# A new order of the round and of the end in a layer-1 FFN laid out by hand over 32 images

## The chip, the cores and the metric

The kernel runs on one core of one Trainium2 chip. The metric is device microseconds (us) of one execution; lower is better. A core has TensorE (PE in the profile; its weight loads are PEld), VectorE (DVE), ScalarE (ACT), GpSimd (POOL) and SyncE (SP), each with its own instruction queue that runs strictly in order. Here SP only issues DMAs. An instruction that needs another engine's result waits on a semaphore, and everything behind it on its own queue waits too.

## The reference

A two-layer vision tower over 32 images of 256 tokens with 256 features. Everything ahead of the last stage (tokenizer, layer-0 attention and FFN, layer-1 attention) is the same in both kernels. The last stage, the layer-1 FFN, is what the change reorders. Cut to what matters, with B=32 images, 4 heads (NH) of width 64, and 4 experts (NE) per head:

```python
sx = einsum('bsh,ndh->bnsd', x, hl_w) + hl_b            # heads
q  = einsum('bnsd,neod->bneso', sx, wq)                 # four experts' queries per head
k, v = ...                                              # one key and value per head
att = softmax(q @ k.T * d**0.5 + causal)                # 16 attentions per image
out = att @ v
gs  = softmax(out . gate_w + gate_b)                    # gate over the four experts
mixed = sum over experts of out * gs
hn  = layernorm(mixed + resid)                          # first norm
hx  = relu(hn @ fc1_w.T + fc1_b) @ fc2_w.T + fc2_b      # first and second layer
hx  = layernorm(hx + hn)                                # second norm
fg  = softmax(hx . fgate_w)                             # gate over the four heads
h   = h + hx * fg
```

## The kernel before

All 32 images stay in on-chip memory from stage to stage. The layer-1 FFN takes one image at a time, but no engine finishes an image before it begins the next: the work of an image is cut into some 80 pieces (the tuple `PIECES`; pieces are named below by their function, in words), and `ROUND` lists all of them once, each with an offset. In round r the entry `(-k, p)` does piece p for image r + k. So entries with a large k belong to an image that has just come in, those with k = 1 to one about to leave. `order_e` walks the rounds in this order until piece 3 (`heads`) of image 31 has been done; from there on `END` lists every piece that is left, as `(images before the last, piece)`. Both lists are written out by hand or by a planner ahead of time; at run time nothing decides an order, and each engine runs the pieces that are its own in the order of the list.

The way of one image, with the engine of each step:

1. `features_in` (SP): DMA of the image's normed, turned features, tile exT. `heads` (PE), `heads_out` (ACT, tile sx, L1173), and two DMAs that swap its halves (sw, L1179).
2. `experts` 0 and 1, `head_values` (PE), evicted by ACT (tile g, L1206) and DVE (tile ev, L1221).
3. `scores` 0 to 4 (PE), each followed by `exponentials` of the same number (ACT, tile et, L1250, two instructions each).
4. `outputs` 0 to 3 (PE), evicted by `outputs_out` 0 to 7 (ACT, tile eo, L1285).
5. The gate over experts, `mixed`, `summed` (DVE, L1342 to L1394); `squares` 0 (ACT), `squares_sum` 0 (DVE, L1403), `root` 0 (ACT, a Ln and an Exp, L1410 and L1411), `scaled` (DVE, L1421).
6. The turn: `turn_e` transposes 32x32 blocks on DVE (tile eblk, L1428) and writes them to DRAM by DMA (er_turned, L1433); `moved_e` reads them back with two DMAs (fraw, L1440); `turned_e` scales them on ACT (fxT, L1449). Image 31 alone is turned on PE, without DRAM.
7. `first_layer` (PE, the turned rows' first product), `features_moved` (two DMAs fxT to both, L1461), `first_layer_out` (ACT, tile hx, L1487, then four DMAs hx to both, L1490), `second_layer` (PE), `second_layer_out` (DVE, tile ey, L1502).
8. `squares` 1, `squares_sum` 1, `root` 1; the head gate (`head_gate` 0 to 8, small DVE work with one ACT exponential); `last_norm` 0 to 2 (three full DVE passes, L1537 to L1541), 3 and 4 (four DVE instructions each, L1545), 5 (the DMA of the result, L1549). `heads_zero` and `features_zero` count zeros on DVE (L1184).

Eight PSUM banks are handed out in turn in the order of the list (`bank()`), so the ninth bank asked for is the first again, and the product that writes it waits until the engine that evicts the earlier content is done. One round asks for 29 banks. All DMAs of this stage go through SP's one queue in the order of the list; a DMA that has to wait holds back those behind it.

In the round before, `turn_e` of an image stands near the end of a round (entry `(-3, 66)`), `moved_e` opens the next (`(-2, 2)`), `turned_e` and `first_layer` follow in its first half (`(-2, 67)`, `(-2, 69)`) and `second_layer` closes it. `heads` stands just ahead of `second_layer`.

Of the kernel before, what the change touches and what calls it, by code (L numbers as in the profile page):

```python
# [80 lines left out]
def vit_tower(tc, a, out):  # L81
# [1032 lines left out]
    with (  # L1114
# [419 lines left out]
        def last_norm(b, im, i):  # L1534
# [38 lines left out]
            (features_moved,), (count_bad, 0), (count_bad, 1), (count_bad, 2), (count_bad, 3),  # L1573
        )
        ROUND = (
            (-2, 2), (-3, 54), (-1, 72), (-3, 56), (-4, 42), (-6, 4), (-1, 73), (-4, 33), (-1, 74), (-4, 34),
            (-4, 44), (-3, 57), (-4, 45), (-1, 75), (-3, 58), (-3, 59), (-6, 1), (-6, 5), (-4, 43), (-1, 76),
            (-4, 46), (-6, 6), (-5, 16), (-5, 12), (-5, 22), (-1, 77), (-6, 30), (-5, 18), (-2, 67), (-6, 9),
            (-1, 87), (-5, 13), (-4, 47), (-5, 14), (-2, 92), (-2, 69), (-6, 10), (-1, 78), (-5, 19),
            (-6, 11), (-1, 79), (-3, 60), (-4, 48), (-5, 20), (-3, 61), (-6, 7), (-5, 15), (-2, 68),  # L1580
            (-1, 80), (-2, 70), (-1, 89), (-3, 62), (-1, 81), (-4, 49), (-1, 82), (-6, 8), (-1, 88),
            (-3, 63), (-3, 64), (-1, 83), (-5, 31), (-1, 84), (-4, 50), (-5, 32), (-1, 85), (-1, 86),
            (-7, 3), (-8, 0), (-1, 90), (-3, 65), (-5, 21), (-4, 51), (-1, 91), (-5, 41), (-3, 66), (-5, 40),
            (-5, 39), (-4, 52), (-4, 53), (-4, 55), (-2, 71), (-1, 93), (-1, 94), (-1, 95), (-1, 96),
        )
        END = (
            (0, 2), (3, 51), (4, 65), (2, 40), (3, 52), (2, 39), (2, 42), (2, 41), (2, 21), (0, 1), (3, 53),
            (4, 66), (3, 54), (3, 55), (5, 71), (3, 56), (6, 90), (3, 57), (5, 72), (4, 2), (2, 33), (2, 34),
            (0, 4), (5, 73), (5, 74), (3, 58), (2, 43), (5, 75), (2, 44), (3, 59), (1, 15), (5, 76), (2, 46),
            (2, 45), (5, 77), (2, 47), (5, 78), (6, 91), (2, 48), (0, 7), (1, 21), (4, 67), (3, 60), (0, 9),  # L1590
            (2, 49), (3, 61), (4, 92), (2, 50), (5, 79), (4, 69), (0, 10), (0, 5), (0, 8), (2, 51), (3, 62),
            (2, 52), (5, 80), (0, 11), (5, 87), (2, 53), (3, 63), (1, 13), (4, 70), (3, 64), (2, 54),
            (5, 81), (2, 55), (4, 68), (1, 14), (5, 82), (2, 56), (3, 65), (0, 6), (5, 89), (3, 66), (2, 57),
            (1, 19), (1, 16), (1, 12), (1, 20), (0, 12), (5, 83), (5, 88), (4, 71), (1, 18), (1, 22),
            (2, 58), (0, 18), (4, 72), (3, 2), (4, 73), (2, 59), (4, 74), (4, 75), (1, 31), (1, 32), (1, 33),
            (1, 41), (1, 34), (1, 42), (1, 39), (1, 40), (4, 76), (3, 67), (2, 60), (5, 84), (0, 30),
            (5, 85), (3, 69), (2, 61), (5, 86), (5, 90), (1, 44), (3, 68), (0, 13), (1, 43), (2, 62),
            (1, 45), (2, 63), (3, 92), (1, 46), (5, 91), (3, 70), (0, 14), (1, 47), (4, 77), (0, 16),
            (2, 64), (1, 48), (4, 78), (1, 49), (4, 79), (1, 50), (4, 80), (1, 51), (2, 65), (1, 52),
            (1, 53), (4, 81), (2, 66), (0, 22), (0, 15), (4, 82), (0, 19), (1, 55), (1, 54), (0, 20),  # L1600
            (4, 87), (3, 71), (4, 83), (1, 56), (0, 31), (4, 89), (1, 57), (4, 84), (3, 72), (0, 21),
            (1, 58), (0, 32), (0, 40), (3, 73), (4, 85), (1, 59), (4, 88), (1, 60), (0, 41), (0, 42),
            (3, 74), (2, 2), (3, 75), (0, 39), (2, 67), (1, 61), (0, 33), (0, 43), (4, 86), (4, 90), (0, 34),
            (0, 44), (3, 76), (3, 77), (1, 62), (1, 63), (2, 69), (2, 92), (3, 78), (4, 91), (2, 68),
            (2, 70), (1, 64), (1, 65), (3, 79), (0, 46), (0, 45), (0, 47), (3, 80), (1, 66), (0, 48),
            (3, 81), (0, 49), (3, 87), (3, 82), (1, 2), (2, 71), (0, 50), (3, 83), (0, 51), (3, 89), (0, 52),
            (3, 84), (3, 88), (0, 53), (3, 85), (0, 55), (0, 54), (2, 72), (2, 73), (0, 56), (2, 74),
            (3, 86), (0, 57), (2, 75), (3, 90), (2, 76), (0, 58), (3, 91), (1, 67), (2, 77), (0, 59),
            (2, 78), (0, 60), (2, 87), (2, 79), (1, 92), (0, 61), (2, 80), (2, 89), (1, 69), (2, 81),
            (1, 70), (0, 62), (1, 68), (2, 82), (1, 71), (2, 83), (0, 63), (0, 64), (2, 84), (2, 88),  # L1610
            (2, 85), (0, 65), (0, 66), (2, 90), (1, 73), (0, 67), (1, 72), (2, 86), (0, 69), (0, 92),
            (1, 74), (1, 75), (2, 91), (0, 70), (0, 68), (0, 71), (0, 93), (0, 72), (0, 73), (0, 74),
            (0, 94), (1, 76), (0, 75), (1, 77), (0, 76), (0, 95), (1, 78), (0, 77), (0, 87), (0, 78),
            (1, 79), (1, 87), (1, 80), (0, 79), (0, 96), (1, 81), (0, 80), (1, 82), (1, 89), (1, 83),
            (0, 81), (0, 89), (0, 82), (0, 83), (1, 84), (1, 88), (0, 84), (1, 85), (0, 88), (0, 85),
            (1, 86), (1, 90), (1, 91), (0, 90), (0, 86), (0, 91),
        )
        LAST = PIECES.index((heads,))

# [407 lines left out]
```

## Time and profile before

| | us |
|---|---|
| median of 3 runs (1803.8 to 1807.66) | 1806.92 |
| the profiled execution, its own time | 1813.98 |
| its span, first to last instruction | 1812.2 |
| first product of `heads`, image 0 | at 1241.0 |
| the same, image 5 | at 1303.16 |
| the same, image 31, where `END` begins | at 1733.6 |
| last DVE instruction | ends at 1807.6 |

Busy shares of the whole span are PE 97%, DVE 72%, ACT 43%, POOL 25%. The layer-1 FFN is the last 571 us of the span, and the shares there differ from these, so it has to be read by its own stretches: the filling of the pipeline (1241 to 1303), 26 full rounds (to 1733.6) and the end. A matmul's end is modelled, so PE counts as busy while it waits a little; its pace is read from the starts of the products instead.

### The profile page before, as it was taken

To read this page: it belongs to the slowest core of one execution; us is meant where nothing else is said; L and a number is where in the kernel's file an instruction comes from. 1 tells how busy PE (TensorE), PEld (TensorE's weight loads), DVE (VectorE), ACT (ScalarE), POOL (GpSimd) and SP (SyncE) were. 2 spreads that over 40 slices of the span, in tenths; PEclk is the share of its full clock that TensorE was granted. 3 is DMA by queue.
4 is the path that set the end of the run, shared out by engine and by line. 5 is a ranking of instruction groups with operands and counts; after the bars stand their busy time and mean duration, and the time that the engine had idled before them with its cause. 6 is when DMAs were issued, how large, how long until landed. Compare 5 with 4: busy or idle time off the path is not lost.

```text
span 1812.2 us, 43832 instructions
## 1 busy us (share of the span) xinstructions
PE 1763.8 (97%) x18072; PEld 1267.4 (70%) x18072; DVE 1309.8 (72%) x3580; ACT 776.5 (43%) x1607; POOL 445.5 (25%) x506
## 2 busy tenths in 40 slices
PE   9999999999999999999999999999999999999993
PEld 7888566667576676767654555557888888888882
DVE  2335367787878665444458877875699999999998
ACT  0000322222222212121244554555888888888883
POOL 1223234343434335333344433341000000000000
PEclk9999999999999999999999999999999999999995
DMA  8552112121211115233312222112244444444432
GB/s 274 180 154 65 35 30 67 51 72 38 59 47 49 57 50 182 91 119 99 112 57 82 75 88 78 74 71 83 68 114 112 115 111 120 109 118 114 122 99 69
DMA packets 197999, 167.93 MB, mean 93 GB/s; under 512 B 71713, under 2 KB 174881, under 8 KB 197409
## 3 DMA queue, kind: packets, MB, share of 16 engines
q1 hardware_dynamic: 191072, 147.49, 28.4%
q0 software_dynamic: 6144, 16.79, 3.1%
q8 instruction: 144, 2.36, 0.6%
q10 hardware_dynamic: 576, 0.79, 0.2%
q14 instruction: 63, 0.51, 0.1%
HBM read 82.95 MB, written 57.41 MB: 77 GB/s over the span
## 4 chain that ended last, share of the span: by engine, by line
PE 85%; DVE 6%; DMA 4%; ACT 4%; issue 1%; SPq 0%; ACTq 0%; DVEq 0%
PE bank L118 85%; DMA er_turned<-eblk 1%; ACT et L1250 1%; DMA fraw<-er_turned 1%; DMA both<-hx 1%; DVE fout L1545 1%; ACT fxT L1449 0%; DMA patch<-in_patches_dram 0%; PE bank L518 0%; DVE eo L1380 0%; ACT g L1206 0%; DVE eblk L1428 0%; DVE ranges L1403 0%; DVE six L126 0%; ACT eo L1285 0%
## 5 line engine op out<-in xcount | busy, mean ns | idle before, releaser
L118 PE MATMUL bank<-ev,et 64*64 64x72 f32 (+3 forms) x6144 | 186.8, 226 | 0.2
L118 PEld LDWEIGHTS bank<-ev,et 64*64 64x64 f32 (+1 forms) x6144 | 171.6, 135 | 10.9 <-ACT hx L1487 1.2
L118 PE MATMUL bank<-tokW,patch 128*128 128x256 f32 x768 | 170.1, 385 | 2.9 <-DMA patch<-in_patches_dram 2.9
L118 PE MATMUL bank<-g,sw 64*64 64x128 f32 (+2 forms) x1280 | 168.0, 377 | 0.0
L1250 ACT ACTIVATE et<-bank 128x512 f32<-128x512 f32 x320 | 167.4, 624 | 1.2 <-PE bank L118 1.2
L118 PE MATMUL bank<-g,sx 64*64 64x128 f32 (+2 forms) x1280 | 167.6, 377 | 0.0
L118 PEld LDWEIGHTS bank<-tokW,patch 128*128 128x128 f32 x768 | 148.5, 194 | 24.9 <-issue 3.8
L118 PE MATMUL bank<-bxT,w_wuv 128*128 128x512 f32 x300 | 131.4, 592 | 0.0
L869 ACT ACTIVATE hT<-bank,cols 128x512 f32<-128x512 f32 x64 | 43.7, 687 | 187.2 <-PE bank L118 122.3
L118 PE MATMUL bank<-wvo,dm 128*128 128x512 f32 x256 | 114.3, 599 | 0.0
L118 PE MATMUL bank<-w_wo,gT 128*128 128x256 f32 x512 | 113.2, 379 | 0.0
L118 PE MATMUL bank<-attn,bv 128*128 128x256 f32 x512 | 113.1, 379 | 0.0
L118 PE MATMUL bank<-w_w,hT 128*128 128x256 f32 x512 | 112.3, 379 | 0.0
L118 PE MATMUL bank<-xsel,w_w 128*128 128x512 f32 x256 | 111.4, 592 | 0.0
L118 PEld LDWEIGHTS bank<-attn,bv 128*128 128x128 f32 x512 | 97.2, 190 | 19.6 <-issue 7.2
L126 DVE BATCH_NORM_STATS2 six<-h 128x6 f32<-128x256 f32 x256 | 105.7, 413 | 4.4
L118 PEld LDWEIGHTS bank<-w_w,hT 128*128 128x128 f32 x512 | 97.0, 190 | 15.6 <-issue 2.9
L118 PEld LDWEIGHTS bank<-w_wo,gT 128*128 128x128 f32 x512 | 97.2, 190 | 13.4 <-DVE gT L491 0.2
L118 PE MATMUL bank<-w_wuv,bxT 128*128 128x512 f32 x240 | 105.4, 592 | 0.0
L1285 ACT COPY eo<-bank 128x280 f32<-128x280 f32 x256 | 89.3, 396 | 36.4 <-PE bank L118 36.4
L118 PEld LDWEIGHTS bank<-bxT,w_wuv 128*128 128x128 f32 x300 | 57.0, 190 | 64.9 <-issue 64.1
L118 PEld LDWEIGHTS bank<-g,sx 64*64 64x64 f32 x1280 | 92.6, 133 | 10.1
(288 smaller groups left out, 3572.3 us busy)
## 6 DMA issues: line engine op xcount, KB each, us to landing
patch<-in_patches_dram SPq DMA_DIRECT2D x31, 768.0 KB
exT<-normed SPq DMA_DIRECT2D x32, 256.0 KB
sw<-sx SPq DMA_DIRECT2D x64, 128.0 KB
er_turned<-eblk SPq DMA_DIRECT2D x31, 256.0 KB
fraw<-er_turned SPq DMA_DIRECT2D x62, 128.0 KB
both<-fxT SPq DMA_DIRECT2D x62, 128.0 KB
both<-hx SPq DMA_DIRECT2D x124, 64.0 KB
out_dram<-fout SPq DMA_DIRECT2D x31, 256.0 KB
```

Of the source, the lines that this page charges most:

```text
L118: nc.tensor.matmul(o, lhsT, rhs, start=first, stop=last)
L126: nc.vector.bn_stats(six, x)
L869: nc.scalar.activation(s.hT[:, m, :], p, AF.Gelu_apprx_tanh, bias=col("b1", m))
L1250: nc.scalar.activation(t2[:, r, :], p, AF.Exp)
L1285: nc.scalar.copy(im.o[:, g * OC : (g + 1) * OC], p[:, 0:OC])
L1545: nc.vector.scalar_tensor_tensor(f[:, g, :], f[:, g, :], im.gate[:, i - 3, n : n + 1], H[b][:, i - 3, d], ALU.mult, ALU.add)
```

## The change

`ROUND` and `END` are replaced; no piece and no instruction is added, removed or changed in shape. Offsets now reach from -10 to -1 where they reached from -8 to -1: `features_in` is three rounds and more ahead, and the last part of an image (from the gate over heads on) ends one round later. The start of the list is another point of the same cycle; as a cycle, PE's pieces keep their order but for `heads`, which now stands ahead of `scores` 3 and `outputs` 0 and 1 instead of behind them. `turn_e` stands in the middle of a round (`(-4, 66)`), `moved_e` later in it (`(-4, 2)`), and `turned_e` and `first_layer` in the first quarter of the next (`(-3, 67)`, `(-3, 69)`).

```diff
         ROUND = (
-            (-2, 2), (-3, 54), (-1, 72), (-3, 56), (-4, 42), (-6, 4), (-1, 73), (-4, 33), (-1, 74), (-4, 34),
-            (-4, 44), (-3, 57), (-4, 45), (-1, 75), (-3, 58), (-3, 59), (-6, 1), (-6, 5), (-4, 43), (-1, 76),
-            (-4, 46), (-6, 6), (-5, 16), (-5, 12), (-5, 22), (-1, 77), (-6, 30), (-5, 18), (-2, 67), (-6, 9),
-            (-1, 87), (-5, 13), (-4, 47), (-5, 14), (-2, 92), (-2, 69), (-6, 10), (-1, 78), (-5, 19),
-            (-6, 11), (-1, 79), (-3, 60), (-4, 48), (-5, 20), (-3, 61), (-6, 7), (-5, 15), (-2, 68),
-            (-1, 80), (-2, 70), (-1, 89), (-3, 62), (-1, 81), (-4, 49), (-1, 82), (-6, 8), (-1, 88),
-            (-3, 63), (-3, 64), (-1, 83), (-5, 31), (-1, 84), (-4, 50), (-5, 32), (-1, 85), (-1, 86),
-            (-7, 3), (-8, 0), (-1, 90), (-3, 65), (-5, 21), (-4, 51), (-1, 91), (-5, 41), (-3, 66), (-5, 40),
-            (-5, 39), (-4, 52), (-4, 53), (-4, 55), (-2, 71), (-1, 93), (-1, 94), (-1, 95), (-1, 96),
+            (-1, 84), (-6, 22), (-4, 59), (-5, 47), (-3, 67), (-2, 75), (-4, 60), (-7, 9), (-5, 48),
+            (-6, 13), (-4, 61), (-3, 92), (-6, 18), (-7, 10), (-6, 14), (-5, 49), (-7, 11), (-3, 69),
+            (-4, 62), (-5, 50), (-5, 51), (-6, 19), (-1, 87), (-4, 63), (-7, 7), (-5, 52), (-8, 3), (-1, 85),
+            (-1, 89), (-3, 70), (-4, 64), (-5, 53), (-2, 76), (-1, 88), (-4, 65), (-4, 66), (-5, 54),
+            (-6, 20), (-7, 8), (-6, 15), (-1, 90), (-2, 77), (-1, 86), (-7, 30), (-5, 55), (-5, 56),
+            (-1, 91), (-6, 21), (-6, 31), (-8, 4), (-4, 2), (-2, 78), (-5, 57), (-6, 32), (-3, 71), (-6, 41),
+            (-6, 39), (-2, 79), (-2, 80), (-6, 33), (-3, 72), (-2, 81), (-3, 73), (-6, 40), (-10, 0),
+            (-6, 42), (-2, 82), (-3, 68), (-5, 58), (-6, 34), (-6, 43), (-6, 44), (-8, 1), (-8, 5), (-7, 16),
+            (-3, 74), (-6, 45), (-2, 83), (-7, 12), (-6, 46), (-8, 6), (-1, 93), (-1, 94), (-1, 95),
+            (-1, 96),
         )
         END = (
-            (0, 2), (3, 51), (4, 65), (2, 40), (3, 52), (2, 39), (2, 42), (2, 41), (2, 21), (0, 1), (3, 53),
...
-            (1, 86), (1, 90), (1, 91), (0, 90), (0, 86), (0, 91),
+            (0, 1), (7, 85), (7, 89), (1, 30), (5, 70), (4, 64), (3, 53), (2, 20), (7, 88), (4, 65), (1, 8),
+            (2, 15), (2, 31), (3, 55), (3, 54), (4, 66), (3, 56), (7, 86), (2, 32), (3, 57), (7, 90), (0, 4),
...
+            (1, 88), (1, 85), (0, 88), (0, 84), (1, 90), (0, 85), (1, 86), (0, 90), (1, 91), (0, 86),
+            (0, 91),
         )
```

`END` has 305 entries before and 332 after. The pieces that `END` holds more of than before are, on DVE: one `heads_zero`, one `features_zero`, one `last_norm` 0, two of `last_norm` 1, two of `last_norm` 2, one of `last_norm` 3, two of `last_norm` 4 and one set of the small head-gate steps; on PE: `scores` 3, `outputs` 0 and `outputs` 1 of one image.

The numbers of the pieces named most: 2 `moved_e`, 3 `heads`, 4 `heads_out`, 15 `scores` 3, 20 `exponentials` 2, 31 to 34 `outputs` 0 to 3, 64 and 76 `root` 0 and 1, 66 `turn_e`, 67 `turned_e`, 69 `first_layer`, 70 `first_layer_out`, 71 `second_layer`, 86 to 91 `last_norm`, 92 `features_moved`.

## The prediction

> **What bounds the kernel now.** I read the stretches of the last stage first, because shares of the whole span say nothing of it. Columns: stretch, length, busy us of PE, PEld, DVE, ACT, POOL with counts, granted clock, DMA share, GB/s.
>
> ```profile
> core 0: us, PE busy (x) PEld busy (x) DVE busy (x) ACT busy (x) POOL busy (x), PEclk, DMA share, GB/s
> 1241.00:1303.16 62.16, 60.97 (x1521) 53.47 (x1519) 34.91 (x96) 49.26 (x113) 2.40 (x4) 1.00 0.27 73
> 1303.16:1733.62 430.46, 426.14 (x10820) 363.58 (x10817) 409.36 (x1224) 361.73 (x911) 0.00 (x0) 1.00 0.44 114
> 1733.62:1812.20 78.58, 46.33 (x1016) 36.33 (x1012) 71.31 (x233) 40.83 (x106) 0.00 (x0) 0.75 0.31 84
> ```
>
> Two regimes. In the 26 full rounds PE sets the pace and DVE is close behind (409 of 430). In the end PE has 46 of 79 to do and DVE 71, and DVE's last instruction ends at 1807.6, 74 after the start: there DVE is the bound, with next to no idle time. So a microsecond of DVE work moved from the rounds into the end costs a microsecond.
>
> Next, how even the rounds are. The starts of `heads` lie 16.26 or 16.27 apart in the quiet rounds (1536.44, 1552.70), but 17.7 in others (1418.80 to 1436.49). 26 quiet rounds would take 422.9; they took 430.46: **7.6 us are stalls**. The chain of waits through one of the long rounds shows which:
>
> ```profile
> 1420.12 0.65 DVE eblk L1428
> ...
> 1420.79 5.02 DMA er_turned<-eblk
> ...
> 1425.83 0.62 SPq L1440
> ...
> 1426.50 3.62 DMA fraw<-er_turned
> ...
> 1430.22 0.82 ACT fxT L1449
> ...
> 1431.09 2.64 PE bank L118 x44
> ```
>
> From the end of the turn (1420.77) to fxT on ACT 9.45 pass, through two DMAs. ACT stood 1.32 at fxT and PE 1.02 behind it. In quiet rounds fxT starts at its place in ACT's queue with the data already there. ACT's queue allots 8.0 us from the end of the turn to fxT (1404.51 to 1412.48, 1337.66 to 1345.63); the slow cases take 8.5 to 9.5. SP's queue of this round shows why the first DMA was slow: two others of 256 KB stand just ahead of it.
>
> ```profile
> 1419.01 0.58 SPq L1144 DMA_DIRECT2D exT<-normed  x1
> 1419.69 0.48 SPq L1549 DMA_DIRECT2D out_dram<-fout  x1
> 1420.79 0.36 SPq L1433 DMA_DIRECT2D er_turned<-eblk  x1
> 1425.83 1.29 SPq L1440 DMA_DIRECT2D fraw<-er_turned  x2
> ```
>
> Last, ACT's queue in a quiet round, because the new order has to be laid against it. 1542.20 is where `outputs` 3 ends on PE.
>
> ```profile
> 1542.20 0.69 ACT L1285 COPY eo<-bank 128x280 f32<-128x280 f32 x2 [0.46 <-PE bank L118]
> ...
> 1543.51 1.07 ACT L1206 COPY g<-bank 128x512 f32<-128x512 f32 x2
> 1544.46 2.08 ACT L1250 ACTIVATE et<-bank 128x512 f32<-128x512 f32 x4
> 1546.38 0.86 ACT L1449 ACTIVATE fxT<-fraw,cols 128x512 f32<-128x512 f32 x1
> 1547.09 2.11 ACT L1250 ACTIVATE et<-bank 128x512 f32<-128x512 f32 x4
> 1549.00 0.93 ACT L1487 ACTIVATE hx<-bank,cols 128x256 f32<-128x256 f32 x2
> ```
>
> ACT runs without a break from 1542.2 to the end of hx at 1549.93, and `outputs` 0 (begun 1549.75) stops for 0.14 in its fourth product, whose bank that hx frees. So even the quiet round is held by this ACT chain through a bank, by a hair.
>
> **The change, part by part.** No instruction is added. What moves:
>
> 1. *The turn.* PE's work between `turn_e` and `first_layer` of an image grows by `scores` 3 and `outputs` 0 and 1: 0.97 and 2.95 by the starts (1548.78, 1549.75, 1552.70), 3.9 us. Measured from the end of `outputs` 3: DVE should finish the turn near 9.0, and fxT's place in ACT's new queue is 2.9 into the next round, at about 19.1, so 10.1 are allotted against the 9.5 of the slowest seen. On SP, exT and the 256 KB of the result now stand behind er_turned, not ahead; ahead of it stand the four hx DMAs (64 KB each, issued in 2.1 to 2.4), ahead of fraw the result and the two sw DMAs, all with work behind them that is not due for 5 us or more. `moved_e` waiting on SP holds back only `features_in`, due more than a round later. The four hx DMAs themselves gain: from hx to `second_layer` 5.1 are left where 4.7 were. I take all 7.6 of stall as gone in the profiled execution.
>
> [...]
>
> 2. *The round itself.* I lay ACT's new queue from the end of `outputs` 3, with starts back to back as in the rows above (et 0.478, g 0.477, hx 0.357, fxT 0.71, the square 0.52, Ln 0.35 and Exp 0.115): `outputs_out` 6 and 7, then `experts_out` 0 once PE is through at 1.0; 1.97 `exponentials` 4; 2.93 fxT; 3.63 `exponentials` 0; 4.59 the square; 5.11 `exponentials` 1; 6.07 the gate's Exp, 0.14; 6.20 hx; 6.92 `root` 0 and 1; 7.9 `exponentials` 2, whose first instruction ends at 8.55. PE is ready for `scores` 3 at 0.91 + 1.90 + 0.57 + 1.88 + 0.43 + 0.86 + 1.92 = 8.47 and needs the bank that this instruction frees. So the wait moves from `outputs` 0 to `scores` 3 and is about 0.1 again. From there PE needs 0.97 + 2.8 + 1.10 + 2.75 = 7.6 to the end of the next `outputs` 3: a round of 16.2, against 16.265. Bounds: PE alone, 16.1, and, should DVE hold up a `root` or the square, 16.5. I take 16.2: 26 x 0.065 = 1.7 us gained, between -4 and +6. DVE has 15.5 to do a round (409.36 over 26.5), and gets to what ACT waits for some 0.6 us ahead.
>
> 3. *The end.* At `heads` of image 31 PE has 3.75 less behind it than before (`scores` 3, `outputs` 0 and 1, pieces of 0.95 + 1.4 + 1.4), so `END` begins 3.75 earlier. But DVE has more in front of it: two zero counts (1.21), one `last_norm` 0 (0.60), two of 1 (1.20), two of 2 (1.29), three of 3 and 4 (12 x 0.196 = 2.35), head gate less one softmax step (0.65): **7.3 us**, all in the stretch that DVE bounds. The pace of the last kind, eight in 1.57 from start to start, is in the rows of the end:
>
> ```profile
> 1804.36 1.64 DVE L1545 SCALAR_TENSOR_TENSOR fout<-fout,fgate,h 128x64 f32<-128x64 f32 x8
> 1805.93 1.64 DVE L1545 SCALAR_TENSOR_TENSOR eblk<-eblk,fgate,h 128x64 f32<-128x64 f32 x8
> ```
>
> Nothing hides this: the work went out of the filling, where DVE is idle 44% of the time (34.9 busy of 62.2) and nobody gains by its having less. Net +3.5. On top come new waits of DVE: the one tile fout is free again only when the result of the image before has left; in the old end 3.1 us of DVE work lie between at the least, in the new one 2.6 and 2.9; and fxT of images 29 and 30 follow their turns by 8 to 9 us in ACT's queue with a square and a `root` behind them that DVE needs at once. I take 1.2, from 0 to 3.
>
> [...]
>
> 4. *The filling.* The same products in the same order: 0, give or take 1.
>
> **The sum** for the profiled execution: -7.6 - 1.7 - 3.75 + 7.3 + 1.2 = -4.6: its span 1812.2 becomes 1807.6, its own time 1809.4. It stands 7.1 above the median of 1806.92, about as much as its stalls, so the timed runs may hold fewer of them; nothing shows how many. I take 5.5 of 7.6, which makes -2.5: **1804.4 us**, a gain of 0.14%. A measurement of this kernel can tell about 0.2% (3.6 us) from no change, so the likeliest result lies just inside that band, which ends at 1803.3 and 1810.5.
>
> **The rivals.**
>
> *More is gained.* The bank wait falls away and PE's own 16.1 sets the round (-4.3 instead of -1.7), and the timed runs hold all the stalls: -3.75 - 7.6 - 4.3 + 8.5 = -7.2, 1799.8. For it: the stalls are seen in one round of three. Against: ACT's chain fits with nothing to spare.
>
> *The stalls belong to the profiled execution.* Timed runs hold 2: -2 - 1.7 + 3.5 + 1.2 = +1.0, 1808. For it: the 7.1. Against: the timed runs differ among themselves by 3.9 us, which something that varies must cause.
>
> *Slower: ACT's chain is late at `scores` 3.* `root` 0 and 1 now stand between hx and `exponentials` 2, each a Ln that its Exp must wait for, and `root` 0 needs a DVE sum that needs an ACT square. If DVE, at 95% busy, gets there 0.4 late, every round pays it. At a round of 16.56 it is +7.7 instead of -1.7: 1814. The sum without the round's gain is -0.8, so it decides (slower by over 3.6) from a round of 16.43 on, 26 x 0.17 = 4.4. Against: the 0.6 of lead.
>
> *It doesn't do what it says.* The wait at fxT stays, because SP issues er_turned late behind hx. Half of the stalls stay: 1807.
>
> **How the numbers follow.** The likeliest case 0.50 (own range 1801 to 1807.5, four tenths of it below 1803.3); more is gained 0.16; stalls of the profile alone 0.08; late at `scores` 3 0.19; the wait stays 0.07. Faster: 0.20 + 0.16 = 0.36. Slower: 0.19 and a little of the two small ones, 0.22. Same: 0.42. The range, from the gain's side to half of the slow case: 1799 to 1812.
>
> **What would show it.** fxT waiting for fraw gone from the waits of the rounds; rounds of `heads` even at 16.2; `scores` 3, not `outputs` 0, waiting for ACT et; 26 rounds in 421; `END` some 82 us from `heads` of image 31 to the last DVE instruction. It is wrong if rounds are above 16.4, or if the end takes under 78 or over 85.

## The result, and the profile after

The changed kernel takes 1802.12 us (median of 9 runs, 1800.96 to 1804.33), the kernel before on the same chip 1806.66 (9 runs, 1803.8 to 1809.64): a ratio of 0.9974, with a 95% interval of 0.9966 to 0.9982. That is 0.26% faster, inside the range given, 2.3 us below the predicted time, and just past the 0.2% line on the far side of which the likeliest case had been laid.

The last stage by stretches, as it was shown of before (stretch, length, busy us of PE, PEld, DVE, ACT, POOL with counts, granted clock, DMA share, GB/s), from `heads` of image 0, of image 5 and of image 31:

```profile
1237.40:1296.61 59.21, 58.02 (x1408) 48.91 (x1406) 32.91 (x91) 45.62 (x106) 2.40 (x4) 1.00 0.30 78
1296.61:1715.12 418.51, 418.40 (x10819) 352.53 (x10817) 400.94 (x1199) 358.30 (x909) 0.00 (x0) 1.00 0.45 116
1715.12:1799.70 84.58, 48.89 (x1128) 38.36 (x1126) 78.03 (x262) 44.72 (x117) 0.00 (x0) 0.79 0.31 84
```

The filling is 2.9 shorter, the 26 rounds are 11.9 shorter, and the end is 5.7 longer by its last DVE instruction (1794.79, which is 79.67 after the start of `END`; before 73.95). PE now fills the rounds to 418.40 of 418.51. Twenty-five rounds are 16.08 long and one is 16.51. The whole stage is 9.2 shorter up to its last DVE instruction. What is left behind that, the DMA of the last result, takes 4.9 where it took 4.6 (4.3 to 6.3 over all traces, in no relation to the change). Another 3.6 by which the profiled executions differ had gone before `heads` of image 0, in stages that the change doesn't touch.

The waits of the 26 rounds (engine and line, what it waited for, us in total, times, longest), first two of the kernel before:

```profile
ACT eo L1285 <- PE bank L118: 28.7, 52, 0.7
...
ACT fxT L1449 <- DMA fraw<-er_turned: 4.6, 6, 1.3
```

and then the changed kernel:

```profile
ACT eo L1285 <- PE bank L118: 45.5, 52, 1.6
...
PEld bank L118 <- ACT gate L1367: 10.0, 26, 0.4
...
PEld bank L118 <- ACT et L1250: 8.6, 26, 0.3
```

The row of fxT waiting for fraw is gone. ACT now waits 45.5 for `outputs` where it waited 28.7: it has become the engine that waits for PE. The third row looks like the wait that was forecast at `scores` 3. It will turn out to be none.

SP's queue in a quiet round, in which the turn ends at 1604.94:

```profile
1602.70 2.86 SPq L1490 DMA_DIRECT2D both<-hx  x4
1605.66 0.53 SPq L1433 DMA_DIRECT2D er_turned<-eblk  x1
1606.67 0.38 SPq L1549 DMA_DIRECT2D out_dram<-fout  x1
1607.58 1.11 SPq L1179 DMA_DIRECT2D sw<-sx  x2
1608.77 2.39 SPq L1440 DMA_DIRECT2D fraw<-er_turned  x2
1611.22 0.60 SPq L1144 DMA_DIRECT2D exT<-normed  x1
```

The order is as it was laid: er_turned is held back 0.7 by the four issues of hx, and the two DMAs of 256 KB now stand behind it. But fraw is not issued sooner: the result and the two sw DMAs, which wait for ACT's sx, stand ahead of it, and from the end of a turn to the issue of fraw 4.0 us pass in the middle case, where it was 3.1 in the kernel before. What keeps fxT from waiting here is the distance: from the end of a turn to fxT on ACT 10.06 pass in nearly every round, 2.1 more than before, without a gap on ACT.

In the end, two waits of those that had been expected (the first was 2.0 before, the second did not appear):

```profile
ACT fxT L1449 <- DMA fraw<-er_turned: 3.8, 1, 3.8
...
DVE fout L1537 <- DMA out_dram<-fout: 1.0, 1, 1.0
```

### The profile page after: what moved, and what is told of

The parts are those of the page before. It is cut to its first block, busy times and chain, and to the rows that moved or that the text cites. A ratio compares the mean times of both kernels' runs of the same rounds, so it can differ in the third digit from the quotient of the medians.

```text
span 1799.7 us, 43777 instructions
## 1 busy us (share of the span) xinstructions
PE 1753.4 (97%) x18072; PEld 1252.0 (70%) x18072; DVE 1300.9 (72%) x3580; ACT 773.5 (43%) x1607; POOL 444.4 (25%) x506
## 3 DMA queue, kind: packets, MB, share of 16 engines
q1 hardware_dynamic: 191072, 147.49, 28.7%
## 4 chain that ended last, share of the span: by engine, by line
PE 91%; DVE 6%; ACT 1%; DMA 1%; issue 0%; SPq 0%; DVEq 0%; ACTq 0%
PE bank L118 91%; DVE fout L1545 1%; DVE eo L1380 1%; DMA patch<-in_patches_dram 0%; DVE dx L842 0%; PE bank L518 0%; DVE six L126 0%; DVE ranges L1403 0%; ACT dex L950 0%; DVE dxB L199 0%; DVE two L1388 0%; DVE junk L1184 0%; DMA fraw<-er_turned 0%; DVE fout L1537 0%; DVE dz L996 0%
## 5 line engine op out<-in xcount | busy, mean ns | idle before, releaser
L118 PE MATMUL bank<-ev,et 64*64 64x72 f32 (+3 forms) x6144 | 181.5, 226 | 0.7 <-ACT et L1250 0.3
L1250 ACT ACTIVATE et<-bank 128x512 f32<-128x512 f32 x320 | 172.2, 600 | 4.3 <-PE bank L118 4.2
L1285 ACT COPY eo<-bank 128x280 f32<-128x280 f32 x256 | 84.8, 404 | 49.9 <-PE bank L118 49.9
L118 PEld LDWEIGHTS bank<-g,sw 64*64 64x64 f32 x1280 | 86.3, 133 | 15.2 <-ACT et L1250 9.0
```

The source lines that it names most:

```text
L118: nc.tensor.matmul(o, lhsT, rhs, start=first, stop=last)
L1250: nc.scalar.activation(t2[:, r, :], p, AF.Exp)
L1285: nc.scalar.copy(im.o[:, g * OC : (g + 1) * OC], p[:, 0:OC])
```

## The experiments

Each is compared with the kernel before on its own chip. "Trace" gives filling, 26 rounds and end (to the last DVE instruction) of one execution.

**How many stalls does an execution of before usually hold?** The kernel before, word for word, a second time.

> The kernel before once more, word for word, for a second profile of it. Theory A (the stalls at fxT are a standing part of this order): 26 rounds again take 430, some 7 us above 26 quiet rounds of 16.265, and the profiled execution is again some 7 us above the timed ones. Theory B (the first profiled execution was an unlucky one): 26 rounds take 424 to 427 (1 to 4 us of stalls), and its own time lies among the timed runs. Against the kernel before: ratio 1.000 within 0.002.

1804.71, a ratio of 0.9995 [0.9986, 1.0004]. Trace: 62.16, 426.31, 73.91. Rounds are 16.25 when quiet, so the stalls are 426.31 - 26 x 16.25 = 3.8 us, not 7.6:

```profile
ACT fxT L1449 <- DMA fraw<-er_turned: 2.5, 4, 1.1
```

The execution profiled first was an unlucky one, in this stage and, by 4.5 us, ahead of it (`heads` of image 0 at 1241.0 there, 1236.5 here). Two executions show that the stalls vary (a third with the same order of DMAs, below, has 6.3); how often each size comes they don't tell.

**Is it the order on SP or the distance?** First the order alone, in the kernel before: the DMAs of the result and of exT go behind er_turned.

```diff
-            (-7, 3), (-8, 0), (-1, 90), (-3, 65), (-5, 21), (-4, 51), (-1, 91), (-5, 41), (-3, 66), (-5, 40),
+            (-7, 3), (-1, 90), (-3, 65), (-5, 21), (-4, 51), (-5, 41), (-3, 66), (-1, 91), (-8, 0), (-5, 40),
```

> The kernel before with two entries of the round moved: the DMA of the result (-1, 91) and features_in (-8, 0) are issued behind er_turned instead of ahead of it. PE's, ACT's and DVE's orders and the distance from turn to first product stay. Theory A (er_turned is slow because two DMAs of 256 KB stand just ahead of it): er_turned lands within 2.1 to 3 us in every round, fxT never waits for fraw, the long rounds are gone, 2 to 7 us faster in the profile, 0.1 to 0.2% in the timed runs. Theory B (er_turned is slow by itself from time to time, and only distance helps): long rounds stay about as many, ratio 1.000 within 0.001.

1804.21, 0.9992 [0.9983, 1.0001]. Trace: 62.16, 423.29, 73.65. From the issue of er_turned to that of fraw, which waits for it, 2.2 us now pass in the middle case, where it was 2.9 in the second trace of before. Single ones still take up to 3.6, so "in every round" did not come true. No wait of fxT of 0.2 or more is left in the rounds, which are 3.0 shorter. In the timed runs the gain can't be told from the 0.9995 of the unchanged kernel.

Then the changed kernel with the distance taken back: `turn_e` later, so that 8.4 us lie between turn and fxT instead of 10.1, with SP's new order kept.

```diff
-(-4, 65), (-4, 66), (-5, 54),
+(-4, 65), (-5, 54),
-(-1, 86), (-7, 30),
+(-1, 86), (-4, 66), (-7, 30),
```

> The changed kernel with turn_e moved 1.8 us of DVE work later in the round (behind last_norm 4), so that from turn to fxT some 8.3 us are left, as in the kernel before (8.0), where the changed kernel has 10.1. PE's and ACT's orders stay; on SP er_turned still has only hx's four DMAs ahead of it, and no DMA of 256 KB. Theory A (distance alone cures the stalls): fxT waits for fraw again in some rounds, by up to 1 us, long rounds of 16.3 to 17 come back, 1 to 6 us slower than the changed kernel (1803 to 1808). Theory B (SP's order alone cured them): rounds stay even at 16.08, 1802.

1800.52, 0.9977 [0.9967, 0.9987]. Trace: 59.24, 418.30, 79.04, rounds of 16.08 and no wait of fxT for fraw. So with the new order 8.4 were enough here. Both runs seem to speak for the order, but neither settles it: they are one trace each, the timed runs don't tell them from their neighbours, and a later turn also meets other DMAs on its way. The run of both small edits, further down, speaks against it.

**What made the quiet round 16.26?** In the kernel before, `root` 1 earlier in ACT's queue and `outputs_out` 6 behind it, so that hx ends sooner against `outputs` 0.

```diff
-            (-4, 44), (-3, 57), (-4, 45), (-1, 75), (-3, 58), (-3, 59), (-6, 1), (-6, 5), (-4, 43), (-1, 76),
+            (-4, 44), (-3, 57), (-1, 75), (-1, 76), (-4, 45), (-3, 58), (-3, 59), (-6, 1), (-6, 5), (-4, 43),
```

> The kernel before with one ACT step moved: root 1 (a Ln and an Exp) stands ahead of outputs_out 6 instead of behind it, where ACT stands idle for some 0.4 us a round. Theory A (the quiet round of 16.265 is held by ACT's chain from the end of outputs 3 to hx, through the bank that outputs 0 needs): the chain gets some 0.35 shorter, the wait of 0.14 in the fourth product of outputs 0 goes, quiet rounds of 16.12, 26 x 0.14 = 3.6 us or 0.2% faster, stalls at fxT unchanged. Theory B (PE's own pace sets 16.265): quiet rounds stay at 16.26 to 16.27, ratio 1.000.

1802.87, 0.9985 [0.9978, 0.9992]. Quiet rounds are 16.11, and the stop of 0.13 to 0.14 in `outputs` 0 is gone from the starts of the products: hx ends 13.33 after the start of `heads` instead of 13.49, and the product that started 0.05 behind it, at 13.54, no longer waits. The stalls are as before (425.13 - 26 x 16.11 = 6.3). That ACT's chain up to hx held up the quiet round is shown.

**Does `scores` 3 wait in the changed kernel?** Two runs move ACT's work there both ways. In one, `exponentials` 2 goes behind `experts_out` 1, so that the bank it frees would come free about 1 us later.

```diff
-            (-6, 20), (-7, 8), (-6, 15),
+            (-7, 8), (-6, 20), (-6, 15),
```

> The changed kernel with exponentials 2 moved behind experts_out 1 on ACT (two neighbours change places), so that its first instruction ends 0.95 us later. Theory A (scores 3 needs the PSUM bank that this instruction frees, and has at most 0.1 us to spare): scores 3 starts some 0.85 later in every round, rounds of 16.9 to 17.0, 26 x 0.85 = 22 us or 1.2% slower than the changed kernel (1824). Theory B (ACT has slack there and PE's own pace is all that counts): rounds stay at 16.08, 1802.

In the other, `root` 1 goes behind `exponentials` 2, which so ends earlier.

```diff
-(-5, 53), (-2, 76), (-1, 88), (-4, 65), (-4, 66), (-5, 54), (-6, 20), (-7, 8),
+(-5, 53), (-1, 88), (-4, 65), (-4, 66), (-5, 54), (-6, 20), (-2, 76), (-7, 8),
```

> The changed kernel with root 1 moved behind exponentials 2, so that the bank for scores 3 is freed some 0.45 us sooner. Theory A (PE's own pace already sets 16.08, ACT is just in time): rounds stay at 16.08, the wait of scores 3 for ACT's et goes from the waits, ratio to the changed kernel 1.000 within 0.001 (1802). Theory B (ACT's chain still holds the round): rounds of 15.9 to 16.0, 2 to 4 us faster (1798 to 1800).

1801.31 (0.9965 [0.9951, 0.9979]) and 1800.94 (0.9957 [0.994, 0.9974]); rounds stay at 16.08 in both. In the second the row of `scores` 3 and et stays too (8.3 in 25), which theory A had expected to go. The wait that was forecast at `scores` 3 doesn't exist. In the changed kernel its first weight load and ACT's instruction ahead of it stand so:

```profile
1604.48 0.13 PEld L118 LDWEIGHTS bank<-g,sw 64*64 64x64 f32 x1 [0.33 <-ACT et L1250]
```

```profile
1603.81 1.06 ACT L1250 ACTIVATE et<-bank 128x512 f32<-128x512 f32 x2
1604.76 1.07 ACT L1206 COPY g<-bank 128x512 f32<-128x512 f32 x2
```

and with `exponentials` 2 behind the eviction of g so:

```profile
1604.98 0.13 PEld L118 LDWEIGHTS bank<-g,sw 64*64 64x64 f32 x1 [0.33 <-ACT g L1206]
```

```profile
1604.32 1.05 ACT L1206 COPY g<-bank 128x512 f32<-128x512 f32 x2
1605.26 2.07 ACT L1250 ACTIVATE et<-bank 128x512 f32<-128x512 f32 x4
```

In the second pair `scores` 3 starts at 1604.98, before `exponentials` 2 has begun (1605.26). So it doesn't need that bank. In both kernels the weight loads stand idle for the same 0.33 after `heads`, whichever ACT instruction happens to end just ahead of it, and `heads` takes 1.92 to the next piece in both, as it did in the kernel before, where `second_layer` followed it. The releaser in the brackets is the last event that came, not the one that was needed.

**Which engine bounds which stretch?** The changed kernel without `last_norm` 1, one DVE pass (0.60 from start to start), for images 24 to 31 only, and then for images 0 to 23 only. Both leave out that multiplication for those images.

```diff
-            if i == 1:
+            if i == 1 and b < 24:
```

> The changed kernel without last_norm 1 (the product with the norm's weights, one DVE pass of 0.60 us) for images 24 to 31, all of whose passes lie in the end. This leaves out part of the computation. Theory A (DVE bounds the end throughout): 8 x 0.60 = 4.8 us faster than the changed kernel (1797.3), all of it behind heads of image 31. Theory B (the end is a chain of waits, PE or DMA, and DVE's passes fill its gaps): less than 2 us faster.

```diff
-            if i == 1:
+            if i == 1 and b >= 24:
```

> The changed kernel without last_norm 1 for images 0 to 23, whose passes lie in the filling and in the rounds: 24 x 0.60 = 14.4 us less DVE work, three times as much as is left out of the end in the other kernel. This leaves out part of the computation. Theory A (PE bounds the rounds, so DVE's work there is free): rounds stay at 16.08, 1802 within 1 us. Theory B (DVE, at 96% busy, holds ACT and PE up): rounds of 15.5 to 15.9, 5 to 14 us faster.

Without it in the end: 1796.71, 0.9932 [0.9915, 0.9948]. Without it in the rounds: 1801.63, 0.9961 [0.9947, 0.9975]. The end of the first and the rounds of the second:

```profile
1715.42:1796.01 80.59, 47.74 (x1128) 38.08 (x1126) 73.98 (x254) 45.03 (x117) 0.00 (x0) 0.81 0.33 88
```

```profile
1298.74:1717.89 419.15, 419.08 (x10818) 352.61 (x10816) 386.46 (x1175) 358.65 (x909) 0.00 (x0) 1.00 0.45 116
```

Eight passes fewer take 4.05 off DVE (78.03 to 73.98) and 3.6 off the end (79.67 to 76.08 at the last DVE instruction; 3.0 against the shortest of the other traces of this end, 79.03). The changed kernel itself was not timed on this chip; against the three others of its rounds and end that were (1800.94 to 1801.63) 4.2 to 4.9 are gone. Twenty-four passes fewer take 14.5 off DVE in the rounds (400.94 to 386.46) and nothing off their length. In the rounds DVE's work is free, in the end most of it is paid for.

**Can the gain be had without the longer end?** The kernel before with both small edits above, its reach of eight images kept, timed beside the changed kernel again.

> The changed kernel word for word, timed beside the three others and the kernel before on one chip. Every theory expects what it gave: 0.9974 of the kernel before within about 0.001, rounds even at 16.08, filling 59.2, 26 rounds 418.5, end 79.7. Differences among the four are read against it.

> The kernel before with two small edits of its round: the DMAs of exT and of the result behind that of er_turned on SP, and root 1 ahead of gate work on ACT. Offsets reach as far as before, so the end stays short. Theory A (the parts add as in the traces): rounds even at 16.1 without the wait of fxT for fraw, 26 rounds in 419, filling 62.2, end 73.9, in all 555.0 against 557.4 of the changed kernel: some 2 us faster than the changed kernel, 0.9962 of the kernel before. Theory B (the stalls are small in timed runs, so that the DMA edit is worth nothing there): as root 1 moved alone, 0.9985, 2 us slower than the changed kernel. Theory C (the stalls come back in the quicker round, where turn to fxT is allotted 0.15 less): rounds of 16.1 with single long ones, about 0.9975.

The changed kernel gives 1801.41, 0.9967 [0.9955, 0.9979]; trace 59.24, 419.32, 79.03. The two small edits give 1802.78, 0.9974 [0.9965, 0.9983]; trace 62.17, 422.69, 73.93. The intervals overlap: that one is the better is not shown. The end is short, and quiet rounds are 16.11, but 3.8 us of stalls are back:

```profile
ACT fxT L1449 <- DMA fraw<-er_turned: 2.6, 4, 1.2
```

Theory C came closest. Here 7.77 us are allotted, 7.96 with the order alone. The first row below is er_turned of a long round, with the two big DMAs well behind it in the queue, and 4.0 still pass until fraw can be issued; the last two are of the same kernel one round earlier, where 2.2 pass:

```profile
1655.05 0.37 SPq L1433 DMA_DIRECT2D er_turned<-eblk  x1
1655.46 0.47 SPq L1549 DMA_DIRECT2D out_dram<-fout  x1
1655.98 0.50 SPq L1144 DMA_DIRECT2D exT<-normed  x1
1659.07 1.29 SPq L1440 DMA_DIRECT2D fraw<-er_turned  x2
```

```profile
1638.77 0.37 SPq L1433 DMA_DIRECT2D er_turned<-eblk  x1
...
1640.99 1.29 SPq L1440 DMA_DIRECT2D fraw<-er_turned  x2
```

So the order brings the usual case from 2.9 to 2.2 but leaves late transfers, and whether they stall depends on the distance after all. The run with the order alone got by with two gaps under 0.1 us; a second trace of the rounds of both small edits (the second run with GpSimd, below) has 5.5 of stalls.

What the late transfers have in common stands in the count of DMA packets between the issue of er_turned and that of fraw (queue and kind, packets, MB, share of the DMA engines' time). For the long round above and for the quick one:

```profile
q1 hardware_dynamic: 1035, 0.77, 65.2%
q8 instruction: 1, 0.02, 1.5%
```

```profile
q1 hardware_dynamic: 437, 0.43, 60.6%
```

In the long round one packet of 16 KB comes in between, of a kind that the profile calls instruction; what it carries is not shown. It began 1.98 after er_turned was issued. In the three traces with this order on SP, images 3 to 29, the 33 transfers that met no such packet took 2.1 to 2.2, and all twelve of 3.0 or more had one (of 16 KB, or of 8 KB on another queue) begin 0.6 to 2.1 after their issue. In the three traces with the old order, the 22 with none that began in the first 3 us took 2.1 to 3.1, and all 22 of 3.5 or more had one begin within 2.2. Images 12, 16, 23 and 29 are late in each of the six (2.7 to 4.6), as they would be if these packets came at fixed places of the program.

The long round that the prediction shows is of this kind too. From the issue of er_turned at 1420.79 to that of fraw, in 40 slices of 0.13 us:

```profile
GB/s 223 179 240 329 345 374 378 386 390 374 342 350 358 496 333 325 220 106 16 0 0 0 0 0 0 0 0 0 8 8 8 8 8 16 24 24 0 0 0 0
...
q8 instruction: 1, 0.02, 2.3%
```

Nearly all is moved within 2.4 us. Then no packet begins for 1.1 us, while the one of 16 KB is under way (1.74 to 3.63), and the last few follow it in a trickle, as if one of the DMA engines had been held by it. No run moved these packets, so this stays a reading of the traces and not a cause shown by experiment.

**Can GpSimd take DVE's work in the end?** `last_norm` 1 and 2 on GpSimd, for images 24 to 28 of the changed kernel, and for images 26 to 28 on top of the two small edits.

```diff
-                nc.vector.tensor_tensor(f, f, over(row_e("fn_g"), G8, 1), ALU.mult)
+                (nc.gpsimd if 24 <= b < 29 else nc.vector).tensor_tensor(f, f, over(row_e("fn_g"), G8, 1), ALU.mult)
...
-                nc.vector.tensor_tensor(f, f, over(row_e("fn_b"), G8, 1), ALU.add)
+                (nc.gpsimd if 24 <= b < 29 else nc.vector).tensor_tensor(f, f, over(row_e("fn_b"), G8, 1), ALU.add)
```

> The changed kernel with last_norm 1 and 2 of images 24 to 28 on GpSimd, which has nothing to do in this stage. Theory A (DVE bounds the end from its start): ten passes of 0.60 from start to start less on DVE, the end 79.7 becomes 73.7, 6 us faster. Theory B (the early part of the end is bounded by PE, only the last 40 us by DVE): the images moved lie mostly in the early part, end 77 to 78, 2 us faster. Theory C (GpSimd needs 1.3 a pass, as its additions of 128x512 in earlier stages, holds the one tile fout for longer, and the next image's last_norm 0 waits on DVE): no gain, or slower.

> The kernel before with the two small edits of its round and, for images 26 to 28, last_norm 1 and 2 on GpSimd. Theory A: six passes of 0.60 less on DVE in its end, 73.9 becomes 70.3, in all 551.4: 6 us faster than the changed kernel and 3.6 faster than the two small edits alone, 0.994 of the kernel before. Theory B: half of that, 1.8, because the early part of the end is bounded by PE. Theory C: nothing, since GpSimd is slower and fout is held for longer.

1802.77 (0.9974 [0.9965, 0.9983]) and 1802.94 (0.9974 [0.9964, 0.9985]): no gain by either. The end of the first is 81.0, up 1.3 to 2.0, that of the second 75.1, up 1.2. It comes out as theory C said, but only half for its reason: GpSimd's passes take 1.26 to 1.75, but no wait of DVE for GpSimd at fout is among the waits. GpSimd and then DVE in the first:

```profile
1743.16 1.28 POOL L1541 TENSOR_TENSOR fout<-fout,rows_e 128x512 f32<-128x512 f32 x1 [13.21 <-DVE fout L1537]
1744.53 1.27 POOL L1539 TENSOR_TENSOR fout<-fout,rows_e 128x512 f32<-128x512 f32 x1
```

```profile
1742.95 0.68 DVE L1184 TENSOR_SCALAR_CACHE_REDUCE junk<-fxT 128x512 f32<-128x512 f32 x1
...
1743.55 0.68 DVE L1403 TENSOR_REDUCE ranges<-esq 128x8 f32<-128x512 f32 x1
...
1744.63 1.34 DVE L1349 TENSOR_TENSOR lg<-eo,ranges 128x48 f32<-128x48 f32 x2
```

The DVE instructions with one tensor to read keep their 0.68 beside GpSimd. The one with two, L1349, takes 1.34 for a pair of which one is 0.20 elsewhere, and is done only when GpSimd's pass is. Over the end, the rows L1349, L1394, L1421, L1510, L1523 and L1532, all with two operands in SBUF, hold some 6.7 us more than in the changed kernel (L1349 0.51 each where it took 0.20, L1532 0.37 for 0.16, L1523 0.32 for 0.15), against ten passes of 0.60 that were taken away. DVE's busy time rises by 1.25, from 78.03 to 79.28; where the rest comes from was not traced.

## Why the prediction was right or wrong, point by point

The sum was made for the profiled execution; the pair of second traces stands beside it, because it is nearer to the timed runs:

| | predicted | first traces | second traces |
|---|---|---|---|
| stalls in the rounds | -7.6 (timed -5.5) | 7.7 to 0.4: -7.3 | 3.8 to 1.2: -2.6 |
| pace of 26 rounds | -1.7 | -4.7 | -4.4 |
| `END` begins earlier, filling | -3.75 + 0 | -2.9 | -2.9 |
| `END` itself, new DVE work and waits | +7.3 + 1.2 | +5.7 | +5.1 |
| sum | -4.6 (timed -2.5) | -9.2 | -4.8 |

The second traces, -4.8, fit the timed gains of 4.5 and 5.6 us, in part by luck: with the DMA of the last result, which the sum leaves out and which took 4.3 in the one and 5.7 in the other, they differ by 3.4.

*The turn.* The wait of fxT is gone as forecast, but for one of 0.6 in the second trace, and by the distance that was laid for it, since fraw is issued later after a turn than before. Six other traces of these rounds, with small edits, hold 0.2 to 1.4 of stalls. One reading failed: "SP's queue of this round shows why the first DMA was slow". The two DMAs of 256 KB stand ahead in every round, quiet or not, and cost about 0.7 in the usual case; in the six traces that were read for it, every transfer of 3.5 or more goes with an instruction packet. The size failed too: a timed run seems to hold 3.8 of stall rather than 5.5, and 1.2 of it in long rounds stays. "The stalls belong to the profiled execution" was half right as a rival. Its 2.0 were too few. In the first trace of before 2.1 to 5.0 pass from the issue of er_turned to the issue that waits for it, and the late transfers decide.

*The round.* This step failed: "So the wait moves from `outputs` 0 to `scores` 3 and is about 0.1 again." The wait at `outputs` 0 was rightly read (moving `root` 1 took 0.14 off the round, and the change 0.17 to 0.18), but none took its place. I had counted the banks in the order of the list and taken the eighth back for the one that `scores` 3 needs; with `exponentials` 2 put later nothing moved. PE's own pace, which I had as the lower bound of 16.1, is the round: 2.7 to 3.0 us more gain than I took. That was my rival "more is gained", in the round's part. For the same reason the slower rival (ACT late at `scores` 3) had no ground: even with `exponentials` 2 a whole eviction later nothing is lost.

*The end.* The new DVE work was rightly listed and priced: 6.7 busy us for the 7.3. That DVE bounds the end stands too. What failed is the +1.2 for new waits: the wait for fout came (1.0), fxT's too (3.8, on ACT), yet DVE's idle time in the end fell from 2.6 to 1.6, probably since the longer list leaves it more work to do beside its waits. The error is 2.8 in the first traces, 3.4 in the second. The granted clock has a mean of 0.79 in the end where it was 0.75; in the kernel before it was 1.00 until 1770, then 0.59 to 1790 and 0.50 behind that, while PE had 12.6 us of work in 42.2. The sum gives the clock no time.

*The filling.* Counted with the 3.75, it is -2.9: 0.85 was lost, inside the margin of 1.

Against the timed form of the sum, stalls and filling were too favourable by 2.9 and 0.85, the round and the end too dear by 2.7 and 3.4. That the errors largely cancel is luck, and the remaining 2.3 put the result across the 0.2% line that the likeliest case stood before.

## What to carry to other kernels

A wait that a profile names is the last event before an instruction, not proof that it was needed: where the idle time stays the same as the named engine is moved (0.33 at `scores` 3 in both orders), there was no wait. Before pricing a stall by one execution, compare that execution's own time with the median; the one here, 0.4% high, held twice the stalls of the next. Look at all DMA traffic before blaming the neighbours in one queue. And a deeper pipeline moves work into its end: here 5 us of end were paid for 7 us in the rounds, and two small edits of the old order (which DMA goes first, which of two ACT instructions) got a gain that can't be told from the whole rewrite's.

## What the runs showed of the hardware that had not been expected

GpSimd and DVE did not work side by side where both read two tensors of SBUF: DVE's small two-operand instructions, 0.15 to 0.20 us long otherwise, took as much as 1.2, while reductions (L1403, 0.68), reciprocals (L1342, 0.36 for two, 0.35 in the changed kernel) and reads from PSUM (L1221, 0.48) kept their times. In the trace the small ones end 0.02 to 0.07 behind GpSimd's pass. So a GpSimd pass of 1.26 or more in place of a DVE pass of 0.60 gained nothing here, where such DVE work stands beside it.

In the three traces with the new order in the kernel before, a write of 256 KB to DRAM with nothing big issued just ahead of it let the DMA that waits for it be issued 2.2 us later in the middle case. In all twelve cases in which it took 3.0 to 4.2 instead, a packet of the kind instruction had begun 0.6 to 2.1 us after it was issued. The reverse does not hold: nine that met one 1.8 to 2.0 after their issue took no more than 2.5. That the packet is the cause was not tested.
